# Turning node features between layouts: TensorE transposes exchanged for VectorE transposes and a trip through DRAM

## The chip, the cores and the metric

One Trainium2 chip, one core of it. The metric is the device time of one execution in microseconds, as the median of several runs. All times inside a run come from one profiled execution, counted from the start of its span.

## What is computed

For each of 16 graphs (batches) of 1024 nodes with 128 features, the reference runs four gated layers with residual, and then four convolution layers that are normalised over all batches:

```
h = max(layernorm(x), 0)
for i in range(4):                        # gated layers, one batch at a time
    m = adj^T @ (h @ weight[i])
    r = sigmoid(m @ w_ih_r + h @ w_hh_r + b);  z = sigmoid(m @ w_ih_z + h @ w_hh_z + b)
    n = tanh(m @ w_ih_n + b_in + r * (h @ w_hh_n + b_hn))
    h = (1 - z) * n + z * h
x = x + h * nodemask
h = max(layernorm(x), 0)
for i in range(4):                        # convolution layers
    h = relu(adj @ (h @ W[i]) + b[i]);  h = batch-normalised h over all batches and nodes
out = x + h
```

x arrives with nodes on the rows: x[b] is 1024 x 128. Layer norm needs a node's features in one row; the gates need features on the partitions and nodes along the free axis. So each batch is turned twice: the normed x into `h_in` before the first gated layer, and the last h back to rows before it is added to x. These two turns are what the change is about.

## The kernel before

The kernel has two stages. The gated stage takes up about the first 1229 us and the convolution stage the rest; the change touches the first.

**Tiles.** A batch of h is one tile of 128 partitions (features) by 1024 nodes, worked on in two halves of 512. The adjacency is held as eight row tiles of 128 x 1024. An aggregation (`agg_rows`, matmuls at L525, output `pm`) is 32 matmuls of 128 x 512; a gate step (`gate_step`, L781, matmuls at L790, outputs `g_r`, `g_z`, `g_hn`, `g_xn`) is six matmuls for each half, each in two passes, followed by sigmoid and tanh on ScalarE and five element operations on VectorE (L803 to L812). The aggregate is copied out of PSUM as `m` by ScalarE (L770).

**Streams.** Even batches run as stream A (`sa`), odd ones as stream B (`sb`), one half step apart. `half_step(one, two)` (L856) does the gates of stream `two` and, beside their ScalarE and VectorE work, the aggregation of stream `one`. Each layer of a pair of batches takes two half steps. In the last half step of a batch, `finish` (L829) calls `tail_norm` (L651), which turns the last h with eight TensorE transposes into `pt_x` (L657), adds it to x on VectorE (L660), computes statistics (L609, L610) and stores x to `xmid_d`. The rest of the tail, the second norm and the store to `ymid_d`, is the function `rest`, which the next half step calls. `finish` then calls `take` (L736), which makes the prepared batch current and issues its eight row loads (`load_rows`, L577, DMA at L581) on SP.

**The coming batch.** `ahead` (L817) acts by the number of layers done: at 1 it loads the coming x by a POOL DMA (L540), at 2 it norms it into `y_in` (`prepare`, L727), at 3 it turns `y_in` with eight TensorE transposes into `pt_in` (L647), and ScalarE copies the result to `h_in` (`turn`, L639, L648). The first aggregation of a batch works on `y_in` itself, so only the gates of the first layer and their final blend (L810) read `h_in`.

**Beside that.** `look_on` (L838) has POOL copy the coming adjacency inside DRAM (`copy_rows`, L572), cast the current rows to bf16 (L594), and SP turn them with DMA transposes (L595), and VectorE check the rows' low bits ("looks", L589). SP also carries the row loads.

**Order.** In this part SP and POOL keep the order in which the program issues their instructions (`manual_schedule`, L995). TensorE, VectorE and ScalarE are ordered by the planner, which may put a ready instruction ahead of an earlier one. `behind(ins)` (L683) puts the instructions issued inside it behind `ins` on the engine of `ins`. Tiles come from pools with a fixed number of buffers: x has 4, h has 7, `half` (2 KB a partition) has 8, `adjT` has 1.

The calls at the change of batch, as they stand:

```python
one.agg_step(0)
if halfway:
    halfway()
if one.rest:
    with behind(two.last_act):
        one.rest()
    one.rest = None
two.ahead()
one.look_on(two)
one.agg_step(1)
two.finish()
```

In the convolution stage `load_adjT` (L1018) reads the turned adjacency back as bf16 and widens it: into `half` tiles (`packed`) for even batches and into the `adjT` tile (`block`) for odd ones.

Of the kernel before, what the change touches and what calls it, by code (L numbers as in the profile page):

```python
# [8 lines left out]
F32 = mybir.dt.float32  # L9
# [5 lines left out]
ALU = mybir.AluOpType  # L15
AX = mybir.AxisListType
P = 128
# [324 lines left out]
def exact_path(  # L342
# [191 lines left out]
    with ExitStack() as st:  # L534
# [42 lines left out]
        def load_rows(b):  # L577
# [4 lines left out]
                ts.append(t)  # L582
            return ts

        def look(b, row, j, part=0):

            lows = row.bitcast(U16).rearrange("p (n t) -> p n t", t=2)[:, :, 0]
            k = (b + part * B) * NB + j
            nc.vector.tensor_reduce(low[:, k : k + 1], lows, axis=AX.X, op=ALU.max)  # L589
# [46 lines left out]
            norm_scale(nt, 0, NB)  # L636
            norm_blocks(xt, y, nt, range(NB))

        def turn(y, name, hT=None, func=AF.Copy):  # L639

            if hT is None:
                hT = work.tile([P, N], F32, tag="h", name=f"h_{name}", bufs=7)
            for hf in range(NH):
                pt = tmp(f"pt_{name}_{hf}")
                for q in range(BH):
                    k = hf * BH + q
                    nc.tensor.transpose(pt[:, q * P : (q + 1) * P], y[:, k * P : (k + 1) * P], ident)  # L647
                nc.scalar.activation(hT[:, hf * HALF : (hf + 1) * HALF], pt, func)  # L648
            return hT

        def tail_norm(b, xt, hT):  # L651

            for hf in range(NH):
                pt = tmp(f"pt_x{b}_{hf}")
                for q in range(BH):
                    k = hf * BH + q
                    nc.tensor.transpose(pt[:, q * P : (q + 1) * P], hT[:, k * P : (k + 1) * P], ident)  # L657
                for q in range(BH):
                    k = hf * BH + q
                    nc.vector.scalar_tensor_tensor(  # L660
                        xt[:, k, :],
                        pt[:, q * P : (q + 1) * P],
                        maskT[:, b * NB + k : b * NB + k + 1],
                        xt[:, k, :],
                        ALU.mult,
                        ALU.add,
                    )
            nt = norm_stats(xt, f"mid{b}")
            if b + 1 < B:
                y = work.tile([P, N], F32, tag="h", name=f"y_mid{b}", bufs=7)  # L670
            else:
                y = xt.rearrange("p k c -> p (k c)")
            nc.gpsimd.dma_start(xmid_d[b].rearrange("(k p) c -> p k c", p=P), xt)

            def rest():
                norm_apply(xt, y, nt)
                nc.gpsimd.dma_start(ymid_d[b], y)

            return rest
# [10 lines left out]
        class Stream:  # L690


            def __init__(self, first):
                self.b, self.i, self.rest, self.tag = first, 0, None, "AB"[first % 2]
                self.opened = None

            def open(self, xt):

# [28 lines left out]
            def prepare(self, b, xt):  # L727
                y = work.tile([P, N], F32, tag=f"y{self.tag}", name=f"y_in{b}", bufs=1)
                norm(xt, y, f"in{b}")
                self.ready = b, xt, y  # L730

            def prepare_turn(self):
                b, xt, y = self.ready
                self.ready = xt, y, turn(y, f"in{b}")

            def take(self):  # L736
                self.xt, self.y, self.hT = self.ready
                self.rows = load_rows(self.b)
                self.looks = 0

            def split_step(self):
                nm = f"{self.b}_{self.i}"
# [38 lines left out]
            def gate_step(self, hf, between=None):  # L781
                i, nm = self.i, f"{self.b}_{self.i}_{hf}"
                if hf == 0 and not self.opened:
                    self.new = work.tile([P, N], F32, tag="h", name=f"h{nm}", bufs=7)
                cols = slice(hf * HALF, (hf + 1) * HALF)
                hin, m = self.hT[:, cols], self.m[hf]
                pr, pz, phn, pxn = self.opened or (acc(t, f"{t}{nm}") for t in ("g_r", "g_z", "g_hn", "g_xn"))

                def part(po, wT, g, rhs, start, stop):
                    nc.tensor.matmul(po, wT[:, i, g * C : (g + 1) * C], rhs, start=start, stop=stop)  # L790

                part(pr, w_hhT, 0, hin, True, False)
                part(pr, w_mT, 0, m, False, True)
                if not self.opened:
                    part(phn, w_hhT, 2, hin, True, True)
                part(pxn, w_mT, 2, m, True, True)
                part(pz, w_hhT, 1, hin, True, False)
                part(pz, w_mT, 1, m, False, True)
                self.opened = None
                r = work.tile([P, HALF], F32, tag="r", name=f"r{nm}")  # L800
                z = work.tile([P, HALF], F32, tag="z", name=f"z{nm}")
                nc.scalar.activation(r, pr, AF.Sigmoid, bias=brz[:, 3 * i : 3 * i + 1])  # L802
                nc.vector.scalar_tensor_tensor(r, phn, b_hn(i), r, ALU.add, ALU.mult)  # L803
                nc.vector.tensor_add(r, pxn, r)  # L804
                if between:
                    between()
                nc.scalar.activation(r, r, AF.Tanh, bias=b_in(i))  # L807
                self.last_act = nc.scalar.activation(z, pz, AF.Sigmoid, bias=brz[:, 3 * i + 1 : 3 * i + 2])  # L808
                ho = self.new[:, cols]
                nc.vector.tensor_sub(ho, hin, r)  # L810
                nc.vector.tensor_mul(ho, ho, z)
                self.last_dve = nc.vector.tensor_add(ho, ho, r)  # L812
                if hf == NH - 1:
                    self.hT = self.new
                    self.i += 1

            def ahead(self):  # L817

                if self.b + 2 >= B:
                    return  # L820
                if self.i == 1:
                    self.next_x = load_x(self.b + 2, nc.gpsimd)
                if self.i == 2:
                    with behind(self.last_act, self.last_dve):
                        self.prepare(self.b + 2, self.next_x)
                if self.i == 3:
                    self.prepare_turn()

            def finish(self):  # L829

                if self.i == L:
                    assert self.looks == NB
                    self.rest = tail_norm(self.b, self.xt, self.hT)
                    self.b, self.i = self.b + 2, 0
                    if self.b < B:
                        self.take()

            def look_on(self, two):  # L838

                if self.i == 0:  # L840
                    return
                if self.i == 1:
                    if self.b + 2 < B:
                        copy_rows(self.b + 2)
                    adjT = turned_tile(f"adjT{self.b}")
                    for j in range(NB):
                        transpose_rows(self.b, self.rows[j], j, adjT)
                    nc.gpsimd.dma_start(adjT_d[self.b], adjT)
                if two.i == 2 and two.b + 2 < B:
                    return  # L850
                with behind(two.last_dve):
                    for j in range(self.looks, min(self.looks + 4, NB)):
                        look(self.b, self.rows[j], j)
                        self.looks += 1

        def half_step(one, two, gated=None, halfway=None):  # L856
# [9 lines left out]
            one.agg_step(0)  # L866
            if halfway:
                halfway()
            if one.rest:
                with behind(two.last_act):  # L870
                    one.rest()
                one.rest = None
            two.ahead()
            one.look_on(two)
            one.agg_step(1)
# [119 lines left out]
        with tc.manual_schedule(engines={mybir.EngineType.Pool, mybir.EngineType.SP}):  # L995
# [4 lines left out]
            sb.gate_step(0)  # L1000
            sb.gate_step(1)
            with tc.issue_after(sb.last_act.ins):
                sa.rest()
            sb.finish()


# [10 lines left out]

    def load_adjT(b, i):  # L1018
        ts = []
        block = turned_tile(f"block{b}_{i}") if b % 2 else None  # L1020
        for j in range(NB):
            t = block[:, j, :] if b % 2 else half_tile(f"packed{b}_{i}_{j}")
            nc.sync.dma_start(t, adjT_d[b][:, j, :])
            r = row_tile(f"wide{b}_{i}_{j}")
            if j % 3 == 1:
# [115 lines left out]
    def fetch_x(b):  # L1141
# [6 lines left out]
                t = t.rearrange("p l c -> p (l c)")  # L1148
                hs.extend(t[:, k * HALF : (k + 1) * HALF] for k in range(3))
        elif b == B - 1:  # L1150
            hs = [half_tile(f"xo_h{k}").bitcast(F32) for k in range(8)]
            row = keep.tile([P, N], F32, tag="row", name="xo_row", bufs=12)
            wide = turned_tile("xo_wide").rearrange("p a n -> p (a n)").bitcast(F32)
            hs.extend(t[:, k * HALF : (k + 1) * HALF] for t, n in ((row, 2), (wide, 8)) for k in range(n))
        else:
            return
        xo.extend(hs[k : k + 2] for k in range(0, len(hs), 2))
# [10 lines left out]
    for b in range(B):  # L1168
# [4 lines left out]
        if waiting:  # L1173
            last = first_weights(*waiting, stats)
            if b == 1:
                with tc.issue_after(last.ins):
                    sb.rest()
        if b == B - 1:
            hw_next = raw_split(1)
        aggregate(pm, hw, rows, 1)  # L1180
# [115 lines left out]
```

## Time and profile before

| what | value |
|---|---|
| median of 3 runs | 1840.81 us (1840.02 to 1841.91) |
| the profiled execution's own time | 1840.61 us |
| its span | 1838.8 us |
| transposes `pt_x` (L657) and `pt_in` (L647) | 128 each, 16.7 and 16.6 us of TensorE busy time |
| ScalarE copy to `h_in` (L648) | 32, mean 595 ns |
| VectorE add of the turned h (L660) | 128, mean 343 ns, from PSUM |
| VectorE element operation of a half from SBUF (L810) | 96, mean 777 ns (minimum near 0.69 us) |
| row loads (L581) | 112, 512 KB each, median 5.8 us from issue to landing |
| DMA | 256,280 packets, 381.21 MB |

An engine's busy time is the union of its instructions. The chain of waits is followed back from the last instruction of a window, at each step to what released it. A DMA's time to landing runs from its issue to the event that reports it complete; the issuing engine goes on meanwhile, unless a later instruction of its own waits.

### The profile page before, as it was taken

What the parts mean: (1) busy time and instruction counts of PE and PEld (TensorE: products, weight loads), DVE (VectorE), ACT (ScalarE), POOL (GpSimd) and SP (SyncE); (2) the same over time, 40 slices, a digit from 0 to 9 for tenths busy, and PEclk for the clock granted to TensorE, in tenths of its full rate; (3) what the DMA queues carried; (4) which work ended last, traced back from release to release, by engine and by line L of the source; (5) the groups of instructions that cost most, each with busy time, mean ns of one, the idle gap of its engine ahead of it and who ended that gap; (6) DMA issues with size and microseconds to landing.
All of it is one profiled execution on the core that took longest, in us unless ns stands there. A gap on an engine that the chain in (4) does not pass through costs nothing.

```text
span 1838.8 us, 21960 instructions
## 1 busy us (share of the span) xinstructions
PE 1821.5 (99%) x7326; PEld 1254.2 (68%) x7326; DVE 1225.6 (67%) x2244; ACT 1035.8 (56%) x1577; POOL 285.0 (15%) x378
## 2 busy tenths in 40 slices
PE   9999999999999999999999999999999999999997
PEld 6566666656566666666565666667778888888886
DVE  7656667567666766766766757676666666666665
ACT  5544454553545554445355353467777767767764
POOL 4131320230231042023023013011100000000011
PEclk9999999999999999999999999999999999999999
DMA  7189775575486386567557546349876676767676
GB/s 264 39 247 317 209 229 195 162 206 192 159 233 180 126 233 178 196 172 217 218 159 206 178 145 172 103 159 332 291 248 228 212 256 204 257 209 260 210 249 242
DMA packets 256280, 381.21 MB, mean 207 GB/s; under 512 B 149932, under 2 KB 155856, under 8 KB 252320
## 3 DMA queue, kind: packets, MB, share of 16 engines
q1 hardware_dynamic: 237968, 245.95, 44.2%
q0 software_dynamic: 17664, 133.53, 20.4%
q8 instruction: 59, 0.97, 0.2%
q14 instruction: 61, 0.50, 0.1%
q10 hardware_dynamic: 528, 0.26, 0.0%
HBM read 287.39 MB, written 117.44 MB: 220 GB/s over the span
## 4 chain that ended last, share of the span: by engine, by line
PE 94%; DVE 2%; ACT 2%; issue 1%; DMA 1%; SPq 0%; POOL 0%; DVEq 0%; ACTq 0%; POOLq 0%
PE pm L525 24%; PE pc_m L525 12%; PE g_r L790 11%; PE g_z L790 11%; PE pc_g_r L525 6%; PE pc_g_z L525 6%; PE g_hn L790 6%; PE g_xn L790 6%; PE hw_c L500 4%; PE hw_g L498 2%; PE pw_g_hn L1096 1%; PE pw_g_xn L1096 1%; PE pt_in L647 1%; PE pt_x L657 1%; PE pc_g_r L510 1%
## 5 line engine op out<-in xcount | busy, mean ns | idle before, releaser
L525 PE MATMUL pm<-row,ghw 128*128 128x512 f32 x2048 | 515.6, 406 | 0.1
L525 PEld LDWEIGHTS pm<-row,ghw 128*128 128x128 f32 x2048 | 383.2, 188 | 112.6 <-issue 36.9
L525 PE MATMUL pc_m<-wide,chw 128*128 128x512 f32 x1024 | 246.0, 395 | 0.0
L525 PEld LDWEIGHTS pc_m<-wide,chw 128*128 128x128 f32 x1024 | 190.5, 188 | 42.3 <-issue 4.3
L807 ACT ACTIVATE r<-r,vecs 128x512 f32<-128x512 f32 x128 | 92.3, 721 | 216.8 <-DVE r L804 216.8
L525 PE MATMUL pc_g_r<-wide,chw 128*128 128x512 f32 x464 | 187.0, 403 | 0.3 <-ACT chw L502 0.3
L525 PE MATMUL pc_g_z<-wide,chw 128*128 128x512 f32 x464 | 180.9, 390 | 0.0
L594 POOL CAST half<-row 128x1024 bf16<-128x1024 f32 x128 | 139.7, 1108 | 250.9 <-DMA adjT<-half 169.6
L1028 DVE CAST wide<-packed 128x1024 fp32r<-128x1024 bf16 x160 | 110.0, 692 | 74.5 <-PE pc_m L525 56.4
L1028 DVE CAST wide<-block 128x1024 fp32r<-128x1024 bf16 x160 | 110.2, 691 | 73.2 <-PE pc_g_z L525 40.2
L503 DVE TENSOR_TENSOR ghw<-hw_g,ghw 128x512 fp32r<-128x512 f32 x96 | 62.0, 686 | 129.7 <-ACT ghw L502 129.5
L1026 ACT CAST wide<-block 128x1024 fp32r<-128x1024 bf16 x96 | 100.6, 1048 | 59.3 <-PE pc_m L525 34.3
L803 DVE SCALAR_TENSOR_TENSOR r<-g_hn,vecs,r 128x512 f32<-128x512 f32 x128 | 95.4, 745 | 56.8 <-ACT r L802 31.3
L1026 ACT CAST wide<-packed 128x1024 fp32r<-128x1024 bf16 x96 | 100.7, 1049 | 55.6 <-PE pc_g_z L525 23.7
L790 PE MATMUL g_r<-m,w_mT 128*128 128x512 f32 x256 | 130.7, 592 | 0.0
L790 PE MATMUL g_z<-m,w_mT 128*128 128x512 f32 x256 | 130.7, 592 | 0.0
L790 PE MATMUL g_xn<-m,w_mT 128*128 128x512 f32 x256 | 130.7, 592 | 0.0
L589 DVE TENSOR_REDUCE low<-row 128x1 f32<-128x1024 uint16 x112 | 128.6, 1210 | 0.0
L808 ACT ACTIVATE z<-g_z,brz 128x512 f32<-128x512 f32 x128 | 87.1, 680 | 71.0 <-PE g_z L790 71.0
L770 ACT COPY m<-pm 128x512 f32<-128x512 f32 x128 | 68.8, 586 | 101.3 <-PE pm L525 101.2
L802 ACT ACTIVATE r<-g_r,brz 128x512 f32<-128x512 f32 x128 | 87.7, 685 | 60.3 <-PE g_r L790 59.5
L810 DVE TENSOR_TENSOR h<-h,r 128x512 f32<-128x512 f32 x96 | 74.6, 777 | 62.4 <-ACT r L807 62.4
(176 smaller groups left out, 2764.0 us busy)
## 6 DMA issues: line engine op xcount, KB each, us to landing
packed<-adjT_d SPq DMA_DIRECT2D x256, 256.0 KB, 5.9
block<-adjT_d SPq DMA_DIRECT2D x256, 256.0 KB, 5.4
raw<-in_adj_dram POOLq DMA_DIRECT2D x112, 512.0 KB, 11.6
row<-raw SPq DMA_DIRECT2D x112, 512.0 KB, 5.8
adjT_d<-adjT POOLq DMA_DIRECT2D x16, 2048.0 KB, 7.9
xmid_d<-x POOLq DMA_DIRECT2D x16, 512.0 KB, 4.8
y<-ymid_d POOLq DMA_DIRECT2D x16, 512.0 KB, 5.1
ymid_d<-y_mid POOLq DMA_DIRECT2D x15, 512.0 KB, 3.0
```

The source lines that it names most:

```text
L500: nc.tensor.matmul(pt[:, q * P : (q + 1) * P], src, w, start=True, stop=True)
L525: nc.tensor.matmul(pm[hf], hw[s][:, j * P : (j + 1) * P], rows[j][:, hf * HALF : (hf + 1) * HALF], start=(j == 0 and s == 0), stop=(j == N ...
L589: nc.vector.tensor_reduce(low[:, k : k + 1], lows, axis=AX.X, op=ALU.max)
L594: nc.gpsimd.tensor_copy(t, row.bitcast(F32))
L790: nc.tensor.matmul(po, wT[:, i, g * C : (g + 1) * C], rhs, start=start, stop=stop)
L802: nc.scalar.activation(r, pr, AF.Sigmoid, bias=brz[:, 3 * i : 3 * i + 1])
L803: nc.vector.scalar_tensor_tensor(r, phn, b_hn(i), r, ALU.add, ALU.mult)
L807: nc.scalar.activation(r, r, AF.Tanh, bias=b_in(i))
L808: self.last_act = nc.scalar.activation(z, pz, AF.Sigmoid, bias=brz[:, 3 * i + 1 : 3 * i + 2])
L810: nc.vector.tensor_sub(ho, hin, r)
L1026: nc.scalar.copy(r, t)
L1028: nc.vector.tensor_copy(r, t)
```

## The change

The TensorE turn of the coming x goes for all batches that are prepared by `ahead` (2 to 15), and that of the last h for all batches that another one follows in their stream (0 to 13). Instead:

- VectorE transposes the 32 x 32 blocks of each half (`blocks_out`) into a `half` tile; SP stores it to a DRAM tile (`exchange_out`) and loads it back in four DMAs (`exchange_in`), one for each group of 32 partitions, in pieces of 128 floats.
- `h_in` then holds its nodes in another order inside each half. The first layer's gates read it through `by_nodes` and write PSUM through `four_ways`; the blend does the same.
- `take` issues the outward half for the coming batch, `finish` that for the last h. The next half step issues the loads (`arrive`), the one after it runs `tail_norm`, and the one after that `rest`: two half steps later than before.
- `ahead` loads both streams' coming x when stream A has two layers done, and norms when a stream has three. The looks give way at three instead of two.
- In the convolution stage `block` and `packed` change places between even and odd batches, and `fetch_x` takes its tiles in another order.

```diff
+        def exchange_out(t, name):
+            d = rawd.tile([P, HALF], F32, tag="cross", name=f"cross_{name}", bufs=8)
+            nc.sync.dma_start(d, t)
+            return d
+
+        def exchange_in(d, t):
+            src = d.rearrange("(t r) (s x) -> s r t x", t=4, s=4)
+            for s in range(4):
+                nc.sync.dma_start(t[s * 32 : (s + 1) * 32, :].rearrange("r (t x) -> r t x", t=4), src[s])
...
+        def by_nodes(cols):
+            return cols.rearrange("c (q k i) -> c k q i", q=4, i=32)
+
+        def four_ways(cols):
+            return cols.rearrange("p (k a c) -> p k a c", a=4, c=32)
+
+        def blocks_out(src, name):
+            ds = []
+            for hf in range(NH):
+                t = half_tile(f"t_{name}_{hf}").bitcast(F32)
+                last = nc.vector.transpose(by_nodes(t), four_ways(src[:, hf * HALF : (hf + 1) * HALF]))
+                ds.append(exchange_out(t, f"{name}_{hf}"))
+            return ds, last
+
+        def tail_norm(b, xt, hT, parts=None):
             for hf in range(NH):
-                pt = tmp(f"pt_x{b}_{hf}")
-                for q in range(BH):
-                    k = hf * BH + q
-                    nc.tensor.transpose(pt[:, q * P : (q + 1) * P], hT[:, k * P : (k + 1) * P], ident)
+                if parts:
+                    pt = by_nodes(parts[hf])
+                else:
+                    pt = tmp(f"pt_x{b}_{hf}")
+                    for q in range(BH):
+                        k = hf * BH + q
+                        nc.tensor.transpose(pt[:, q * P : (q + 1) * P], hT[:, k * P : (k + 1) * P], ident)
+                    pt = four_ways(pt)
...
             def take(self):
-                self.xt, self.y, self.hT = self.ready
+                self.xt, self.y = self.ready
                 self.rows = load_rows(self.b)
-                self.looks = 0
+                self.looks, self.across = 0, True
+                self.hT = work.tile([P, N], F32, tag="h", name=f"h_in{self.b}", bufs=7)
+                return blocks_out(self.y, f"in{self.b}")[0]
...
+                across = self.across and i == 0
+                if across:
+                    hin = by_nodes(hin)
...
                 def part(po, wT, g, rhs, start, stop):
+                    if rhs is hin and across:
+                        po = four_ways(po)
...
-                if self.i == 1:
-                    self.next_x = load_x(self.b + 2, nc.gpsimd)
-                if self.i == 2:
+                if self.i == 2 and self is sa:
+                    for stream in (sa, sb):
+                        stream.next_x = load_x(stream.b + 2, nc.gpsimd)
+                if self.i == 3:
                     with behind(self.last_act, self.last_dve):
                         self.prepare(self.b + 2, self.next_x)
-                if self.i == 3:
-                    self.prepare_turn()
...
             def finish(self):
-                if self.i == L:
-                    assert self.looks == NB
-                    self.rest = tail_norm(self.b, self.xt, self.hT)
-                    self.b, self.i = self.b + 2, 0
-                    if self.b < B:
-                        self.take()
+                if self.i < L:
+                    return
+                assert self.looks == NB
+                args = self.b, self.xt, self.hT
+                self.b, self.i = self.b + 2, 0
+                ins = self.take() if self.b < B else None
+                if not ins:
+                    self.ends = [tail_norm(*args)]
+                    return
+                h_in = self.hT
+                outs, last = blocks_out(args[-1], f"out{args[0]}")
+                parts = [half_tile(f"n_{args[0]}_{hf}").bitcast(F32) for hf in range(NH)]
+
+                def arrive():
+                    for hf in range(NH):
+                        exchange_in(ins[hf], h_in[:, hf * HALF : (hf + 1) * HALF])
+                    for hf in range(NH):
+                        exchange_in(outs[hf], parts[hf])
+                    self.ends.append(lambda: self.ends.append(tail_norm(*args, parts)))
+
+                self.ends = [arrive]
+
+            def end_step(self, *after):
+                if self.ends:
+                    with behind(*after):
+                        self.ends.pop(0)()
...
-                if two.i == 2 and two.b + 2 < B:
+                if two.i == 3 and two.b + 2 < B:
                     return
...
-            if one.rest:
-                with behind(two.last_act):
-                    one.rest()
-                one.rest = None
+            one.end_step(two.last_act)
+            two.end_step(two.last_dve)
             two.ahead()
...
     def load_adjT(b, i):
         ts = []
-        block = turned_tile(f"block{b}_{i}") if b % 2 else None
+        block = None if b % 2 else turned_tile(f"block{b}_{i}")
         for j in range(NB):
-            t = block[:, j, :] if b % 2 else half_tile(f"packed{b}_{i}_{j}")
+            t = half_tile(f"packed{b}_{i}_{j}") if b % 2 else block[:, j, :]
```

## The prediction

> **What bounds the kernel now.** I read the page's first parts, then the chain of waits inside one change of batch, then the tiles that the change takes off TensorE, then engines and DMA step by step through the same stretch.
>
> ```profile
> span 1838.8 us, 21960 instructions
> PE 1821.5 (99%) x7326; PEld 1254.2 (68%) x7326; DVE 1225.6 (67%) x2244; ACT 1035.8 (56%) x1577; POOL 285.0 (15%) x378
> ...
> PE 94%; DVE 2%; ACT 2%; issue 1%; DMA 1%; SPq 0%; POOL 0%; DVEq 0%; ACTq 0%; POOLq 0%
> ```
>
> TensorE is busy 99% of the span and carries 94% of the chain. Work taken off it shortens the run by its own length, unless something else then comes late. The chain while stream A ends its batch (608.6) and stream B ends its own (627.0):
>
> ```profile
> 585.61 0.87 PE pt_in L647 x8
> ...
> 601.30 7.28 PE pm L525 x32
> 608.59 0.87 PE pt_x L657 x8
> 609.46 1.72 PE g_r L790 x4
> ...
> 619.76 7.27 PE pm L525 x32
> 627.03 0.87 PE pt_x L657 x8
> 627.91 1.72 PE g_r L790 x4
> ```
>
> Nothing but matmuls, back to back; one half step is 18.45 us (609.46 to 627.91). Each turn of a batch is 8 transposes and 0.87 us of this chain: pt_in in the middle of an aggregation, pt_x between an aggregation and the gates. The busy times (16.6 and 16.7 us for 128 each, 130 ns a piece) would give 1.04 us a turn, but they count ends that overlap the next matmul, so I take the chain's 0.87.
>
> The other engines in five half steps from the last gates of stream A's batch on; the columns are window, length, busy time (instructions) of PE, PEld, DVE, ACT, POOL, then clock, DMA share, GB/s:
>
> ```profile
> 590.80:609.30 18.50, 18.50 (x67) 11.44 (x66) 14.10 (x19) 7.23 (x14) 0.00 (x0) 1.00 0.59 211
> 609.30:627.70 18.40, 18.40 (x66) 11.35 (x65) 12.12 (x39) 10.75 (x21) 1.47 (x2) 1.00 0.41 164
> 627.70:646.50 18.80, 18.80 (x67) 11.63 (x66) 11.08 (x36) 11.44 (x21) 2.79 (x4) 1.00 0.19 64
> 646.50:665.00 18.50, 18.50 (x65) 11.40 (x64) 13.88 (x16) 7.36 (x12) 6.40 (x11) 1.00 1.01 315
> 665.00:684.00 19.00, 19.00 (x67) 11.61 (x66) 13.28 (x31) 8.62 (x16) 9.45 (x12) 1.00 0.64 134
> ```
>
> VectorE has 4.4 to 7.7 us free in each; the DMA engines have 7.6, 10.9 and 15.2 us free in the first three and nothing in the fourth, where the DRAM copies of adj run.
>
> **What the Trainium skill says.** "VectorE: DVE Perf Modes", section The three transpose paths: VectorE's transpose turns 32x32 blocks only, so the rest needs another path, here the DRAM exchange. "Vector Engine (DVE) Microarchitecture Reference", 3.8: it sustains one element per cycle per lane; at the 0.96 GHz of the first page that is 512/0.96 = 533 ns for a half, an estimate. No transpose of VectorE is in this trace; its other 128x512 f32 operations take 0.69 us, which agrees with one element a cycle and some fixed time. "SBUF — State Buffer", section Door 1: The DMA port swizzle: lines are 16 bytes, and strides that leave a line after one element cost; in PSUM any non-contiguous pattern slows matmuls. The changed gates read h_in in runs of 32 floats (128 bytes) and write PSUM in plain order, so I take them at the old 0.43 us a pass; no row shows it.
>
> **The change part by part.**
>
> *Removed from TensorE.* turn goes for batches 2 to 15 (14), the turn in tail_norm for batches 0 to 13 (14); batches 14 and 15 keep theirs. 28 x 0.87 = 24.4 us, all on the chain. ScalarE loses 28 copies of 0.595 us, which were in its free time: nothing.
>
> *Cover lost.* The pt_x turn stood where ScalarE copies m out of PSUM for the gates that follow. At 608.42 the first turn starts; without it the two passes g_r<-h (0.86 us) start there and end at 609.28, while m is ready at 609.32, behind one cast on ScalarE. At 626.87 they end at 627.73 with m ready at 627.43. I take 0.1 us for each of the 14 ends, 1.4 us; between 0 and 0.6 (a copy) each, so up to 8.
>
> *VectorE.* Four transposes a batch, 56 in all, at 0.69 us (0.55 to 1.4, twice the row for 4-byte data): 2.8 us a batch in the half step of 14.10 busy of 18.5. In it 4.6 us are the looks (L589), which nothing urgent awaits. The 8 scalar_tensor_tensor and 8 + 8 statistics (L660, L609, L610), about 4.3 us, move two half steps on, behind that step's last gate operation, where 11.08 and 13.88 of about 18.6 are busy. The norm of the coming x moves two half steps later, the looks into other steps. All hidden: 0; if VectorE were full it would be a gate's delay, at most 2.8 us a batch.
>
> *SP.* Per batch 4 stores out and 16 loads back (4 per half, 128 pieces of 512 B each). They stand in SP's hand-written order behind this stream's row loads and ahead of the other stream's. issue_after puts no wait on them, because it binds only instructions of ScalarE or VectorE here; what SP waits for is the transposes and the stores' landing. What stands behind: the other stream's 8 row loads, then its own stores and loads, then the DMA transposes of adj. Issue distances of SP in the trace go from 0.36 (block) to 0.91 us (rows); I take 0.5. Stream A: y's transposes run in free VectorE time before 603, its h is complete at 603.5, stores out by 605, landed by 608; 16 loads from 605 to 614. h_in lands by about 613 and is needed at 627. Stream B's row loads then go out at 614 to 621 in place of 602 to 609 and land by 628; its first aggregation starts at 638. Its stores leave at 622, land near 628 (5.8 us, the rows' landing time, since they follow them), its h_in loads go out from 628 to 632 and land by 636; needed at 646 less the 1.7 us saved, 644.6. Slack of 14 and about 8 us: 0.
>
> *DMA engines.* 14 x 2 MB on 381 MB, and 14 x 4 x (128 + 512) = 35,840 packets. Queue 1's own mean is 44.2% of 16 x 1838.8 us over 237,968 packets, 55 ns, so 123 us of all 16 engines, 17.6 per pair of batches. The three half steps hold 33.7 us free: it fits.
>
> *POOL.* The xmid and ymid stores come two half steps later and stand ahead of the copies and casts of the next: casts for adjT begin near 664 instead of 653, and stream B's end near 726 instead of 717. The next row loads on SP come 154 us after 582.9, at 737. Both coming x together wait for the old x to be read, then have two half steps. 0, and the swap of block and packed tiles in the convolution is symmetric: 0.
>
> **The sum.** 1838.8 - 24.4 + 1.4 = 1815.8 span; the profiled execution took 1840.61, 1.8 more than its span, so 1817.6, and the median (1840.81) stands 0.2 above it: 1818.
>
> **Rivals.**
> - *It goes through as summed* (0.62): 1813 to 1823, by 0 to 8 us of lost cover.
> - *Stream B's h_in comes a little late* (0.12): with 0.7 us an issue the 16 loads of A and 8 rows end 5 us later, B's loads 2 us more, and a landing of 6 us eats the rest: 1 to 2.5 us at 7 ends, 7 to 17 us, so 1825 to 1835. For it: one queue in hand-written order with store, wait, load twice. Against it: 8 us of slack.
> - *The saving cancels* (0.05): 3.5 us late at 7 ends (24.4/7), 1837 to 1844.
> - *Slower: SP's convoy* (0.21). If the planner puts h's transposes behind the looks (608 to 611), loads go at the rows' 0.91 us and land in 5.8: A's h loads end at 629, B's rows at 636, B's stores land at 643 and h_in's last at 656, against a need at 644.6 for the first half and 650 for the second. 6 us late x 7 = 42, so 1860. It decides from 3.5 us late per pair on. The same chance covers a planner that reorders TensorE around a transfer it believes slow. For it: 20 small transfers a batch on the queue that feeds the rows. Against: SP waits now for TensorE, not the reverse (rows make TensorE wait 0.2 us in all).
>
> **How the numbers follow.** The likeliest gives 1818. Its own range with the second case is 1813 to 1835; the unknown transposes and strided reads push the low end to 1812 at most, as nothing but the 28 turns leaves the chain. To hold 8 in 10 the range goes up to the cancelling case, 1845. About 0.2% (3.7 us) is what a measurement can tell from no change: faster 0.74, same 0.05, slower 0.21.
>
> **What would show it.** Right: no g_r<-h_in matmul waits for a DMA, half steps at a change of batch last 17.6 us instead of 18.45, pt_x and pt_in keep 16 transposes each, VectorE's transposes near 0.69 us, TensorE still at 99%. Wrong: TensorE idle in front of g_r<-h_in or the first pm of a batch with a DMA as releaser, strided g_r passes over 0.43 us apart, or row loads landing after 638 in this stretch's terms.

## The result, and the profile after

| | before | after |
|---|---|---|
| median | 1840.70 us (4 runs) | 1826.63 us (4 runs, 1825.64 to 1829.0) |
| ratio after/before | | 0.9925, 95% interval 0.9908 to 0.9942 |
| span of the profiled execution | 1838.8 us | 1823.7 us |

The change makes the kernel 14.1 us faster; the forecast of 1818 us is 22.7 below this median of before. The sign and the stated range (1812 to 1845) held; 8.6 us of the gain are missing, and this document is about them.

The page of the kernel after: the span, the busy times, the DMA totals and the chain's shares.

```profile
span 1823.7 us, 22030 instructions
...
PE 1799.9 (99%) x7102; PEld 1229.3 (67%) x7102; DVE 1257.1 (69%) x2300; ACT 1020.5 (56%) x1549; POOL 289.9 (16%) x378
...
DMA packets 296604, 410.61 MB, mean 225 GB/s; under 512 B 154412, under 2 KB 189008, under 8 KB 292640
...
PE 64%; ACT 2%; DVE 2%; issue 1%; DMA 1%; POOL 0%; DVEq 0%; ACTq 0%; POOLq 0%
```

TensorE has lost the 224 transposes (7326 to 7102) and 21.6 us of busy time, but the span fell by only 15.1: 6.5 us more of it are not TensorE work. The page's 99% can't show that: 1821.5 of 1838.8 is 99.1%, 1799.9 of 1823.7 is 98.7%. The chain's shares add up to about 70% here, so its line is not compared with the 94% of before; I read the chain inside a stretch instead. This is the same change of batch as shown of before (start, length, what):

```profile
574.93 5.25 PE pm L525 x23
...
580.79 3.18 ACT y_in L636 x8
583.97 0.47 ACT m L793
584.44 0.04 issue
584.49 1.12 PE g_r L818 x2
...
593.39 6.38 PE pm L525 x28
599.77 1.92 PE g_r L818 x4
...
610.27 7.30 PE pm L525 x32
617.58 1.72 PE g_r L818 x4
```

Two things are to be seen. At 599.77 and 617.58 the gates follow the aggregation directly: the turns `pt_x` are gone as planned. But one half step earlier, at 580.79, the chain leaves TensorE. It goes through eight norm blocks and an `m` copy on ScalarE, which the same stretch of before did not have on it. The table of waits says how often (what waited, for what: us in total, times, longest; PE is TensorE's matmuls, PEld its loading of weights, which overlaps them):

```profile
PE g_r L818 <- ACT m L793: 5.7, 9, 1.8
...
PEld g_r L818 <- ACT m L793: 29.0, 48, 2.6
```

Before, the first of these lines didn't exist, and the second was:

```profile
PEld g_r L790 <- ACT m L770: 11.3, 42, 0.6
```

The stretch by half steps (window, length, busy us of PE, PEld, DVE, ACT, POOL, then clock, DMA share, GB/s):

```profile
584.40:602.10 17.70, 17.61 (x56) 10.52 (x57) 15.01 (x21) 9.60 (x17) 0.56 (x1) 1.00 0.98 346
602.10:619.70 17.60, 17.60 (x58) 10.56 (x57) 9.96 (x15) 5.26 (x9) 0.00 (x0) 1.00 0.77 258
619.70:638.40 18.70, 18.70 (x69) 11.76 (x68) 12.59 (x36) 5.79 (x10) 0.93 (x1) 1.00 0.76 265
638.40:656.80 18.40, 18.40 (x63) 10.84 (x62) 13.33 (x38) 11.06 (x21) 1.93 (x3) 1.00 0.05 20
656.80:675.30 18.50, 18.50 (x66) 11.44 (x65) 16.23 (x23) 12.44 (x22) 6.22 (x11) 1.00 0.99 293
```

No compute engine but TensorE is full in any of them; the DMA engines are in the first and the last (0.98, 0.99), and whether that costs time is tested below. What is late is one instruction at one place, and busy shares don't show that.

To find all such places I measured every half step as the time between the last aggregation matmuls of two successive ones, and took the median over seven pairs of batches for each of the eight half steps of a pair. Half step 0 is the one after stream A hands over to its next batch. "Turns left out" and the last two columns are experiments, described below.

```
half step     before   turns left out   after   norm later   all three edits
    0          18.45       17.80        17.80     17.62        17.80
    1          18.46       17.58        17.58     17.58        17.58
    2          18.45       18.46        18.71     18.74        18.46
    3          18.46       18.45        18.45     18.74        18.45
    4          18.56       18.50        18.46     18.46        18.46
    5          19.64       18.74        18.45     18.45        18.45
    6          19.35       18.46        18.50     18.46        18.46
    7          18.46       18.45        19.18     18.45        18.45
```

18.46 is a half step in which TensorE never stops, and 17.58 is one in half steps 0 and 1, whose aggregation is a first one and has no `hw_g` transposes ahead of it. Before, half steps 0 and 1 held `pt_x` and 5 and 6 `pt_in` (0.87 to 0.89 each), and 5 a wait of some 0.3 besides. After, 0 and 1 are short as forecast, but 7 lasts 0.72 and 2 lasts 0.25 longer than TensorE's own work. Single half steps stand out too: one of 20.57 near 880 us and one of 19.73 near 1118 us, each with a longer wait for `m` (1.81 and 1.01 us). At the first, `m` stands behind the coming norm once more; at the second, in half step 4, behind the norm of the batch that has ended.

The place in half step 7, on ScalarE and on TensorE (start, length, engine, line, what; idle time before it and its releaser in brackets):

```profile
726.76 0.30 ACT L624 ACTIVATE rs_in<-mv_in,eps_t 128x8 f32<-128x8 f32 x1 [3.78 <-DVE mv_in L621]
727.36 0.62 ACT L776 CAST ghw<-y_in 128x512 fp32r<-128x512 f32 x1 [0.29 <-PE pm L525]
727.89 3.18 ACT L636 ACTIVATE y_in<-x,ms_in,rs_in 128x128 f32<-128x128 f32 x8
730.97 1.04 ACT L793 COPY m<-pm 128x512 f32<-128x512 f32 x2
```

```profile
730.15 1.02 PE L818 MATMUL g_z<-h,w_hhT 128*128 128x512 f32 x2
731.58 1.12 PE L818 MATMUL g_r<-m,w_mT 128*128 128x512 f32 x2 [0.41 <-ACT m L793]
```

ScalarE stands idle for 3.78 us because VectorE's statistics of the coming x end late. Then the eight blocks of the norm run, 3.18 us in one piece, and just then the aggregation is ready and `m` has to be copied. The copies stand behind the blocks, and TensorE, which needs `m`, runs out of gates that don't. The gap is 0.41 us; the half step is 0.72 longer. Of the difference 0.26 shows in the chain above: after a gap the first two passes take 1.12 us of it, where two passes in a running stream take 0.86.

### The profile page after: what moved, and what is told of

Same layout as the page of the kernel before. It is cut to its first block, busy times and chain, and to the rows that moved or that the text cites. A ratio compares the mean times of both kernels' runs of the same rounds, so it can differ in the third digit from the quotient of the medians.

```text
span 1823.7 us, 22030 instructions
## 1 busy us (share of the span) xinstructions
PE 1799.9 (99%) x7102; PEld 1229.3 (67%) x7102; DVE 1257.1 (69%) x2300; ACT 1020.5 (56%) x1549; POOL 289.9 (16%) x378
## 4 chain that ended last, share of the span: by engine, by line
PE 64%; ACT 2%; DVE 2%; issue 1%; DMA 1%; POOL 0%; DVEq 0%; ACTq 0%; POOLq 0%
PE pm L525 13%; PE pc_m L525 12%; PE g_r L818 6%; PE g_z L818 6%; PE pc_g_r L525 6%; PE pc_g_z L525 6%; PE hw_c L500 4%; PE g_xn L818 3%; PE g_hn L818 3%; PE hw_g L498 1%; ACT y_in L636 1%; PE pw_g_hn L1144 1%; PE pw_g_xn L1144 1%; PE pc_g_r L510 1%; PE pc_g_z L510 1%
## 5 line engine op out<-in xcount | busy, mean ns | idle before, releaser
L605 POOL CAST half<-row 128x1024 bf16<-128x1024 f32 x128 | 144.1, 1144 | 255.0 <-DMA adjT<-half 148.5
L1124 DVE BATCH_NORM_STATS2 stats<-feat 128x6 f32<-128x512 f32 x128 | 84.1, 686 | 46.9 <-ACT feat L1123 45.8
L842 DVE TENSOR_TENSOR h<-h,z 128x512 f32<-128x512 f32 x128 | 100.4, 784 | 17.5 <-ACT z L836 11.9
```

Source lines behind the costliest of these rows:

```text
L605: nc.gpsimd.tensor_copy(t, row.bitcast(F32))
L1124: nc.vector.bn_stats(stats[:, b * NH + hf, :], dst)
```

## The experiments

Theory A: the missing gain is the coming norm's ScalarE part, which the change moved into half step 7, ahead of `m`'s copies. Rivals: B, the exchange's transfers or SP's queue cost the time; C, the planner orders TensorE worse; D, the turns were worth less than 0.87 us. All experiments start from the kernel after unless said otherwise. Times are medians; the kernel before, measured beside them on the same chip, was at 1840.5 to 1841.1 us.

**Norm later: the norm's statistics stay, its ScalarE part goes to the next half step.**

```diff
-                norm(xt, y, f"in{b}")
+                self.waiting = b, xt, norm_stats(xt, f"in{b}")
...
+            def settle(self, *after):
...
+                with behind(*after):
+                    norm_apply(xt, y, nt)
...
+            one.settle(two.last_act)
             one.end_step(two.last_act)
```

> The changed kernel (1826.6 us), with the norm of the coming x cut in two: its statistics on VectorE stay in the half step where they are, its ScalarE part (square root, eight blocks) goes into the next half step, right behind that step's last gate activation. Theory A (what is missing of the forecast went into copies of m that wait on ScalarE behind the eight blocks of the moved norm): the half step of 19.2 us goes to 18.5, twice it is more, so 5 to 8 us less: 1819 to 1822. Theory B (the missing time is the exchange's traffic and SP's queue) and theory C (the planner puts TensorE's matmuls in a poor order around the transfer): no change, 1825 to 1828.

Measured: 1819.44 us (1818.87 to 1824.28), ratio 0.9883 (0.9867 to 0.99): 7.2 us less than after. Half step 7 is back at 18.45. The line of TensorE's waits for `m`, in this kernel's profiled execution (1824.28 us, the longest of the four):

```profile
PE g_r L826 <- ACT m L801: 2.6, 3, 2.1
```

Nine waits became three, and the seven of half step 7 are gone. The longest of the three, 2.09 us, lies in half step 4 of the last pair, behind the norm of the ended batch. Theory A is shown, for 7.2 us net: half step 3 rose by 0.29 at the same time, and half step 0 fell by 0.18.

**Turns left out: the kernel before, with the 28 turns not computed and nothing put in their place.** `h_in` is then ScalarE's plain copy of the normed x, and the last h is added as it lies.

```diff
-                pt = tmp(f"pt_{name}_{hf}")
-                for q in range(BH):
+                pt = y[:, hf * HALF : (hf + 1) * HALF] if far else tmp(f"pt_{name}_{hf}")
+                for q in () if far else range(BH):
...
+                far = b + 2 < B
+                pt = hT[:, hf * HALF : (hf + 1) * HALF] if far else tmp(f"pt_x{b}_{hf}")
+                for q in () if far else range(BH):
```

> The kernel before (1840.8 us), with the 28 TensorE turns simply left out and nothing in their place: h_in is a plain copy of the normed x, and the last h is added to x without being turned, so that both are wrong layouts for batches 2 to 15 and 0 to 13. No exchange, no moved norm. Theory A (a turn is worth its 0.87 us, the loss is elsewhere): 28 x 0.87 less 1 to 2 us, so 1817 to 1819. Rival D (a turn is worth only about 0.5 us of the run, because other work fills its place): 1826, the same as the changed kernel.

Measured: 1817.62 us (1816.81 to 1818.22), ratio 0.9876 (0.9859 to 0.9892), 23.4 us less than before. This is the forecast's own sum (-24.4 + 1.4 = -23.0), so D falls: the turns were worth what they were priced at.

**Moves only: the kernel before, with the earlier loads, the later norm and the looks' new place, and TensorE's turns kept.**

```diff
-                if self.i == 1:
-                    self.next_x = load_x(self.b + 2, nc.gpsimd)
-                if self.i == 2:
+                if self.i == 2 and self is sa:
+                    for stream in (sa, sb):
+                        stream.next_x = load_x(stream.b + 2, nc.gpsimd)
+                if self.i == 3:
...
-                if self.i == 3:
-                    self.prepare_turn()
...
                     if self.b < B:
+                        self.prepare_turn()
                         self.take()
...
-                if two.i == 2 and two.b + 2 < B:
+                if two.i == 3 and two.b + 2 < B:
```

> The kernel before (1840.8 us) with the moves of the change and none of its exchange: both coming x loaded when stream A has two layers done, norm at three, the looks give way at three, and the TensorE turn of the coming x in the last half step. Theory A: the norm costs more in its new place, 3 to 6 us: 1843 to 1847, with waits of TensorE for the copy of m. Theories B and C: no change, 1840 to 1842.

Measured: 1844.04 us (1842.62 to 1845.49), ratio 1.0016 (1.001 to 1.0023): 3.0 us slower than before, from the moves alone.

```profile
PE g_r L790 <- ACT m L770: 2.9, 7, 0.4
```

The gap of 0.41 is there once in each of the seven pairs, with half step 7 at 19.17. So it comes with the moves, and not from VectorE's transposes or from any transfer of the exchange; that it is the norm among the moves, the experiment with the norm later shows. It costs less in sum than the 7 x 0.72 = 5.0 us, since half step 5's own wait of before (2 us in sum) goes at the same time.

**Before, norm later: the same cut of the norm in the kernel before.**

> The kernel before (1840.8 us) with the same cut of the norm: statistics where they are, the ScalarE part one half step later; the TensorE turns stay. Theory A (the norm held copies of m before the change too, 0.5 us a pair, and costs more since): 3 to 4 us less, 1836.5 to 1838.5. If the loss belongs to the change alone: 1840 to 1842.

Measured: 1840.97 us (1839.74 to 1843.22), ratio 1.0002 (0.9994 to 1.001). A miss: half step 5 fell from 19.64 to 19.35 as A expects, but half step 6 rose from 19.35 to 19.81. "Later" is no good by itself; in half step 6 the blocks were again ahead of an `m` that is needed (ScalarE's blocks, then TensorE's wait):

```profile
568.49 3.19 ACT L625 ACTIVATE y_in<-x,ms_in,rs_in 128x128 f32<-128x128 f32 x8 [1.42 <-DVE ms_in L621]
572.20 1.12 PE L798 MATMUL g_r<-m,w_mT 128*128 128x512 f32 x2 [0.42 <-ACT m L778]
```

**Gates first: in the half step with a batch's first gates, the aggregation stays behind them.** In the kernel after, half step 2 shows another thing, on TensorE itself:

```profile
782.98 1.02 PE L818 MATMUL g_xn<-m,w_mT 128*128 128x512 f32 x2
783.69 2.15 PE L525 MATMUL pm<-row,ghw 128*128 128x512 f32 x7
785.69 1.02 PE L818 MATMUL g_r<-h_in,w_hhT 128*128 128x512 f32 x2
```

Seven aggregation matmuls stand between the first gate product and the others. Nothing forces it: the first half of `h_in` had landed 7.3 to 16.4 us before its first use in all 14 batches.

```diff
+            first = (two.last_pe,) if two.across and two.i == 1 else ()
+            with behind(*first):
-            one.agg_step(0)
+                one.agg_step(0)
```

(The same stands around `agg_step(1)`; `last_pe` is the last gate matmul issued.)

> The changed kernel (1826.6 us), with one order fixed on TensorE: in the half step in which a stream's first gates read h_in, the other stream's aggregation stays behind all of these gates' matmuls. Theory C (the planner believes h_in late, though it lands 7 us and more ahead of its use, and puts matmuls that wait for other things in its place): the third half step of each pair goes from 18.71 to about 18.46, 1.8 us less in seven pairs, 1824 to 1825.5. Theory A alone: no change, 1826 to 1828.

Measured: 1827.8 us (1827.12 to 1829.77), ratio 0.993 (0.9917 to 0.9944). Half step 2 fell to 18.46, but half step 4 rose from 18.46 to 18.91: no gain.

**Both: norm later and gates first.**

> The norm's ScalarE part in the next half step (1819.4 us) together with the gates ahead of the aggregation. In the first of these alone the third and fourth half steps are 18.74 each, 0.29 above a plain one. Theory A and C together: 7 x 0.58 = 4.1 us less, 1814.5 to 1817. If the order costs nothing: 1819.

Measured: 1818.84 us (1818.44 to 1820.42), ratio 0.9881 (0.9866 to 0.9896), above the 1814.5 to 1817 expected. Half steps 2, 3 and 7 are clean, and half step 4, at 18.92, takes 3.2 us. Its ScalarE, and then its VectorE:

```profile
664.48 0.30 ACT L624 ACTIVATE rs_mid<-mv_mid,eps_t 128x8 f32<-128x8 f32 x1
667.27 3.19 ACT L636 ACTIVATE y_mid<-x,ms_mid,rs_mid 128x128 f32<-128x128 f32 x8 [2.49 <-DVE ms_mid L632]
670.37 1.04 ACT L801 COPY m<-pm 128x512 f32<-128x512 f32 x2
```

```profile
664.75 1.21 DVE L600 TENSOR_REDUCE low<-row 128x1 f32<-128x1024 uint16 x1
665.88 0.19 DVE L627 RECIPROCAL rs_mid<-rs_mid 128x8 f32<-128x8 f32 x1
665.99 1.17 DVE L600 TENSOR_REDUCE low<-row 128x1 f32<-128x1024 uint16 x1
667.08 0.16 DVE L632 SCALAR_TENSOR_TENSOR ms_mid<-mv_mid,rs_mid 128x8 f32<-128x8 f32 x1
```

It is the mechanism of half step 7 with another norm, that of the ended batch. Two operations of 0.2 us, which the norm's blocks wait for, stand behind two looks of 1.2 us that nobody waits for. The blocks start 2.49 us late, and `m`'s copies are behind them.

**All three: both, and the looks behind a norm's scale operation of the same half step.**

```diff
-            nc.vector.scalar_tensor_tensor(ms, nt[1][:, k0:k1, 0], -1.0, rs, ALU.mult, ALU.mult)
+            scaled[:] = [nc.vector.scalar_tensor_tensor(ms, nt[1][:, k0:k1, 0], -1.0, rs, ALU.mult, ALU.mult)]
...
-                with behind(two.last_dve):
+                with behind(two.last_dve, *scaled):
```

(`scaled` is emptied at the start of every half step.)

> The version with both edits, and in addition VectorE's four looks (1.2 us each) wait behind the scale operation of a norm that runs in the same half step. Nothing is left out. In the version with both edits the ScalarE blocks y_mid of the last batch's norm waited 2.49 us for ms_mid, because two looks stood ahead of it on VectorE, and m's copies stood behind those blocks; the fifth half step of a pair was 18.92 us where an undisturbed one is 18.46. If this is what holds the fifth half step (theory: m's copies late behind a norm's blocks on ScalarE, whatever makes the blocks late), the fifth goes to about 18.5 us in all seven pairs: -3.2 us, median about 1815.6 us (1814.5 to 1817), and the gaps of g_r<-m behind ACT m at that place are gone. The blocks themselves stay, 3.2 us in front of the copies. Rival: the blocks are in the way even when they start on time, or the looks, now later, hold up VectorE's next split or the gates: the fifth stays near 18.9 us, or another half step takes the 0.4 us, and the median stays within 1 us of 1818.8.

Measured: 1815.96 us (1815.45 to 1816.11), ratio 0.9866 (0.985 to 0.9883). ScalarE at the same place:

```profile
663.09 3.19 ACT L638 ACTIVATE y_mid<-x,ms_mid,rs_mid 128x128 f32<-128x128 f32 x8 [0.47 <-DVE ms_mid L634]
666.78 1.07 ACT L803 COPY m<-pm 128x512 f32<-128x512 f32 x2 [0.50 <-PE pm L525]
```

Now ScalarE waits 0.50 us for the aggregation, and not the reverse. All half steps but 0, which keeps 0.22 us of lost cover, are at TensorE's own length (last column of the table), and the kernel is 10.7 us faster than after and 24.5 faster than before. The blocks still take their 3.2 us on ScalarE; only their start has moved, from 2.49 to 0.47 us of idle time.

**Loads twice: every load of `h_in` issued a second time, into a spare tile.** This was to show whether SP's queue and the DMA engines have the slack that the forecast gave them.

```diff
                         exchange_in(ins[hf], h_in[:, hf * HALF : (hf + 1) * HALF])
+                        spare = work.tile([P, HALF], F32, tag="spare", name=f"spare_{args[0]}_{hf}", bufs=1)
+                        exchange_in(ins[hf], spare)
```

> The changed kernel (1826.6 us), each of the eight loads of h_in done a second time into a spare tile: 112 more DMAs of 64 KB on SP, 7 MB. h_in lies 9.8 us ahead of its use in the changed kernel's trace and a load takes 0.47 us of SP, so all that stands behind moves by 3.8 us. Theories A and C: no change, 1826 to 1828. Theory B (the queue or the DMA engines are what costs): 14 times 1 to 3.8 us, 1840 or more.

Measured: 1850.88 us (1848.38 to 1852.02), ratio 1.0051 (1.0034 to 1.0068): 24 us slower than after. By the number alone this is what B expected (1840 or more). Yet the first half of `h_in` still landed at least 4.4 us ahead of its use, and no `h_in` matmul waited for a DMA. TensorE's order had changed, and with it what it waits for. In half step 3, at 20.28 us, two aggregation matmuls are drawn in among the gates, and the next `g_r` waits for ScalarE to have read the one before:

```profile
218.61 1.00 PE L525 MATMUL pm<-row,ghw 128*128 128x512 f32 x2
221.09 1.12 PE L818 MATMUL g_r<-h,w_hhT 128*128 128x512 f32 x2 [1.48 <-ACT r L830]
```

In half step 1, at 19.01, transposes `hw_g` stand among aggregation matmuls.

**Loads twice, gates first.** The edit of gates first, on the kernel with doubled loads:

> The doubled loads of h_in (1850.9 us) with the gates ahead of the aggregation. Theory C (no transfer came late there either: h_in landed 4.4 us or more ahead of its use, and only the order on TensorE was worse): back to 1824 to 1830. Theory B (the transfers themselves cost): it stays at 1845 to 1851, or rises.

Measured: 1838.83 us (1836.94 to 1840.9), ratio 0.9987 (0.9978 to 0.9995). One edge in TensorE's order gives back 12 of the 24 us, with the same transfers. What the other 12 were was open, so two more versions took the doubled loads on top of all three edits.

**Loads twice, all three edits.**

> The same without the further edge: TensorE's order then differs from the version with all three edits in one place of each of the seven pairs, where A's hw_g (4, 1 and 3 transposes) stand among B's aggregation matmuls instead of behind them. Theory C: the second half step of a pair is about 19.0 us as in the two versions with doubled loads (17.58 without), the others are undisturbed: 7 x 1.4 = 10 us, median about 1826 us (1824 to 1828). Rival (the transfers cost by themselves): other half steps too are above 18.5 us and the median is above 1830.

Measured: 1838.43 us (1834.72 to 1843.25), ratio 0.9987 (0.998 to 0.9994). The place was right, the size not: only half step 1 is disturbed, but it lasts 20.84 and not 19.0 us. The second half's first `hw_g` stands after only eight of the 32 aggregation matmuls. It waits for an `h` that VectorE has not blended yet, and the rest of the aggregation, which could run, waits behind it (TensorE's order, then the sum of these waits):

```profile
184.67 0.60 PE L498 MATMUL hw_g<-ident,h 128*128 128x128 f32 x4
185.03 2.09 PE L525 MATMUL pm<-row,ghw 128*128 128x512 f32 x8
188.94 0.41 PE L498 MATMUL hw_g<-ident,h 128*128 128x128 f32 x1 [1.82 <-DVE h L853]
189.02 1.18 PE L525 MATMUL pm<-row,ghw 128*128 128x512 f32 x2
```

```profile
PE hw_g L498 <- DVE h L853: 13.0, 7, 2.1
```

**Loads twice, order kept: the same, with `hw_g` held behind the aggregation.** TensorE's order is then that of the version with all three edits, instruction by instruction.

```diff
-                one.split_step()
+                one.split_step(*([two.last_pm] if one is sa and one.i == 1 and one.across else []))
...
-                        features_times(None, self.hT, self.hw, g, f"g{nm}")
+                        with behind(*after):
+                            features_times(None, self.hT, self.hw, g, f"g{nm}")
```

(`last_pm` is the last aggregation matmul of a stream.)

> The version with all three edits, h_in's two loads issued a second time into a spare tile that nothing reads (28 transfers of 256 KB more), and one further edge: A's second-layer transposes hw_g stay behind the last aggregation matmul of the half step before, as they stand in the version with all three edits. TensorE's order is then the same, instruction by instruction, as in that version; only some neighbours on VectorE and ScalarE change places. All of the result is computed. Theory C (the 24 us that the doubled loads cost came from the order on TensorE and the waits that follow from it, not from the transfers): about 1816 us (1815 to 1819), every half step at 17.6, 17.8 or 18.46. Rival (the transfers themselves cost: SyncE's queue, the DMA engines or SBUF's ports are held by them): at least 5 us above 1816, with half steps above 18.5.

Measured: 1815.38 us (1814.48 to 1815.53), ratio 0.9858 (0.9842 to 0.9875). With all the doubled transfers in it, the kernel is as fast as without them. So 112 more transfers cost nothing in this kernel, though they used up room: the first half of one `h_in` landed only 1.1 us before its use. The 23 us between these last two versions were order on TensorE. For the 24 us of the first doubled version this is shown for 12, by one edge; the rest is argued from the same kind of places. What makes the planner choose another order when more transfers are in the program no run shows.

## Why the prediction was right in part

The time lies above the likeliest case's own range (1813 to 1823) and inside that of the rival "Stream B's h_in comes a little late" (1825 to 1835), whose mechanism did not occur. That the number fell there is luck.

**Right: the turns.** 28 x 0.87. Half step 1 went from 18.46 to 17.58, and the version without turns gained 23.4 us where the sum says 23.0.

**Right: the lost cover.** Half step 0 is 17.80 and half step 1 17.58 long: 0.22 x 7 = 1.5 us, against 1.4. It falls on the A ends alone, and shows in the chain as g_r x4 taking 1.92 in place of 1.72. The prediction had put 0.1 on each of the 14 ends, so that the sum agrees is in part luck.

**Right: VectorE's transposes.** 0.69 us each was taken, from the other f32 operations of this size, and not the estimate of 533 ns from the skill's one element a cycle; the measured medians are 0.71 (`t_in`) and 0.68 (`t_out`). The line of `t_in` (duration minimum, median, maximum in ns):

```profile
L673 DVE STREAM_TRANSPOSE t_in<-y_in x28: 667/708/712, 119.8 to 1055.8; 128x512 f32<-128x512 f32 x28
```

**Right: strided gates, SP, DMA.** The matmuls that read `h_in` in runs of 128 bytes take 592 ns in the middle, as before:

```profile
L818 PE MATMUL g_r<-h_in,w_hhT x64: 590/592/697, 20.0 to 1086.0; 128*128 128x512 f32 x64
```

A slack of 14 and about 8 us was worked out for `h_in`, and 7.3 to 16.4 us measured; the doubled loads show that twice these transfers is still no limit. One price in it was too low: the stores were to land in 3 to 6 us, and their medians are 11.0 (`cross_in`) and 8.6 us (`cross_out`). The loads of 64 KB, at 2.0 us (median), gave some of that back, and the slack bore the rest. The DMA rivals, B's `h_in` late and SP's convoy, did not occur. On SBUF's lines, for which the prediction drew on the Trainium skill ("SBUF — State Buffer", Door 1: The DMA port swizzle), these runs agree: no slowdown for runs of this length. What it says of patterns in PSUM no run here tests.

**Wrong: "The norm of the coming x moves two half steps later, the looks into other steps. All hidden: 0."** That is the failed step. It was argued from free time on VectorE: 14.1 busy of 18.5, so there is room. But the norm ends on ScalarE, with 3.18 us of blocks in one piece, and ScalarE also carries the copies of `m`, on which TensorE's next gates depend. Free time in a half step says nothing on whether the blocks stand in front of `m`'s copies at the moment when `m` is due. They did, at 7 of 7 pairs, for about 0.72 us in six of them and 2.1 in one; moving them away was worth 7.2 us, with what it changed in other half steps. The norm's delay was seen in the prediction as "a gate's delay, at most 2.8 us a batch", but only for a full VectorE, which was never the case.

**Mis-sized: the planner.** The sum had nothing for another order on TensorE; it was named in the slower rival alone. In the kernel after it costs 0.25 us in half step 2, 1.8 us in seven pairs, and repairing it (with the looks that then come in the way) is worth 3.5 us, 1819.44 to 1815.96, in the version with the norm later, where half step 3 had lost 0.29 us to it too. In the doubled-loads kernels 23 us hung on the place of eight transposes.

The two add up: 7.2 + 3.5 = 10.7 us of waits in the kernel after. The sum of the forecast would have landed at 1818 only because it took over the waits of before, which the version without turns still has (1817.62 - 1815.96 = 1.7 us). 10.7 - 1.7 = 9.0, against the 8.6 missing.

## What to carry to other kernels

When a change moves work off the bound engine's path, ask of every moved instruction which queue it will stand in, and whether the copy that feeds the bound engine stands behind it; a half-empty engine hides work only if the urgent instruction doesn't come last. Let small operations that a chain waits for go ahead of long ones that nobody waits for, and tie down by hand the orders that carry the time, since an edit elsewhere, here 112 loads that nothing reads, may let a planner choose others. And measure stage by stage: one table of half-step lengths showed here what a busy share of 99% before and after could not.

## What the runs showed that I had not expected

A wait of TensorE can cost more than its gap. In the version with doubled loads and all three edits, TensorE stands still for about 1.82 us in each of seven pairs. In three of them the granted clock (the share of TensorE's full clock that it is given) then fell to half, for 3.41 us each (window, length, PE, PEld, DVE, ACT, POOL, clock, DMA share, GB/s):

```profile
188.90:192.40 3.50, 3.46 (x11) 2.78 (x12) 3.50 (x19) 0.59 (x1) 0.93 (x1) 0.52 0.48 134
192.40:193.40 1.00, 1.00 (x6) 0.82 (x5) 1.00 (x7) 0.00 (x0) 0.00 (x0) 0.97 0.91 292
```

These half steps last 22.15 us, the others of the seven 20.57 or, once, 20.84: 1.6 us more for 3.5 us at 0.52. The version's twenty times fit this: the shortest, 1834.72 us, ran at a mean clock of 0.998, the longest, 1843.25 us, at 0.993. That is why the size expected of that version was missed, beside the longer gap. The same happened once with the norm later (a gap of 2.09 us at 1113.9, a half step of 22.50), and did not after a gap of 1.81 us at 880 in the kernel after. In the gated stages of all the traces, ten gaps after the first 60 us reach 1.8 us, and four of them were followed by such a drop; none of the shorter ones was, and there is no other drop there. What decides between the four and the six the runs don't settle. The Trainium skill ("TensorE: Matmul & The Clock Gate", section HAM oscillation — how this bites in real kernels) warns of idle gaps above about 3.4 us. In these runs about half of that was followed by a drop, some of the time; a gap that short is worth removing for this reason too.
